# A graph layer with gathered node rows: five selected tiles in the odd groups, and gathers released by the selection products alone

## The chip, the cores and the metric

The kernel runs on one core of a Trainium2 chip. The metric is the device time of one execution in microseconds (us). The core has a matrix engine (PE, whose weight loads the profile lists apart as PEld), a vector engine (DVE), a scalar engine (ACT), a general engine (POOL), which here only issues indirect loads, and a queue engine (SP) that issues the plain loads and stores. PE writes its products to PSUM; DVE and ACT read them from there.

## The reference, cut to what matters

There are N = 6250 nodes with F = 64 features, and E = 200,000 edges sorted by their destination. Each edge takes the features of its source node, weighs them by nine numbers from a small network on its attributes, goes through a 64 x 9 x 64 tensor, and is summed at its destination; the sum is scaled and shifted by a second small network, added to the node's features and normalised.

```python
w = jax.nn.silu(edge_attr @ W1 + b1) @ W2 + b2
h_src = features[src]
msg = jnp.einsum('ef,em,fmg->eg', h_src, edge_sh * w, W_tp)
agg = jax.ops.segment_sum(msg, dst, num_segments=N) / jnp.sqrt(jnp.float32(AVG_DEG))
emb = jax.nn.silu(c_noise[:, None] @ Wn1 + bn1) @ Wn2 + bn2
gamma, beta = jnp.split(emb, 2, axis=-1)
x = _layernorm(features + agg * (1.0 + gamma) + beta, axis=-1)
```

## The kernel before

The edges lie in tiles of 128, one edge per partition, and 16 tiles make a group; there are 98 groups, numbered 0 to 97. The main loop (L859) runs over i and works on several groups at once: it brings the rows of the source nodes for group i + 2, selects rows for group i + 1, and sums group i into its destinations.

The rows `features[src]` of a tile reach the tile's place in `hs` in one of three ways.

- **Gathered:** an indirect load on POOL (L125), one per tile. This is how most tiles come.
- **Row by row:** in every fourth group from 7 on (`SPG`), the first tile comes by 128 single-row loads on SP (L143).
- **Picked:** the last `picked(g)` tiles of a group are selected on PE from a copy of all node features that lies on the chip. DVE builds a 128 x 896 table of zeros and ones from the tile's keys (`hot_k`, L653, in `hots`); PE multiplies it with the features in 14 products, seven slices times two halves of the number (`pxw`, L668, in `pick`); DVE keeps the right one of seven columns by a masked multiply (`xm`, L678) and a reduction (L681). There are three PSUM tiles for `pxw` and seven tiles for `hot_k`. The keys are loaded with room for five tiles in every group (`Q` = 5), whether or not five are picked.

Between the first pick of group i + 1 and its other picks stand **the small products** (`middle`, L805): the first layer of the edge network for group i + 2 (`hidden`, L594), its second layer for group i + 1 (`second`, L618), in odd i the projection of a pair of groups (`project`, L760), and the products of the gathered rows with the edge weights for group i (`windows`, L708). For odd i from 3 on, `place` (L775) adds two products that put sums at their nodes inside the first pick. Their PSUM tile is the one that `second` writes next, after ACT (`carry`, L781) and DVE (`yt`, L784) have read it. So an odd i is an iteration in which an even group is picked, and it holds more small products; an even i picks an odd group.

The order on each engine is the program's own order. Gathers are set by hand: `beats(i + LEAD, units)` shares the gathers of group i + 2 evenly over a number of units, and `beat(u, mm)` counts u units when a product has been issued; whenever the count passes the next mark, one gather is issued on POOL that waits for just that product. A product of a pick counts 1, and the small products count 4.5 (`hidden`), 3.4 (`second`), 12 (`project`) and 3.3 for every four products of `windows`. The units of an iteration are 14 per picked tile plus 21 in even i and 33 in odd i. What is left at the end of an iteration is issued without a wait (`beats_end`). A gather's wait needs a notice from PE, an update of PE's semaphore that the product carries; ACT and DVE wait on notices of the same semaphore.

Of the kernel before, what the change touches and what calls it, by code (L numbers as in the profile page):

```python
# [22 lines left out]
NBLK = (NT + KB - 1) // KB  # L23
# [5 lines left out]
LEAD = 2  # L29
LB = 2  # L30
Q = 5
J = 7
# [19 lines left out]

def picked(g):

    return Q - 2 if g in (0, NBLK - 1) else Q - (g % 40 != 30)


def tiles(g):
    return min(KB, NT - g * KB)
# [9 lines left out]
def gnn_resnorm_kernel(ctx: ExitStack, tc: tile.TileContext, x, src, dst, dst_row, ea, sh, cn,  # L69
# [18 lines left out]
    with ExitStack() as fast:  # L88
# [495 lines left out]
        def hidden(g, act=True, beside=None):  # L584

            e = ea_t.pop(g)
            p1 = psum.tile([P, 2, 4 * P], F32, tag="p1", name=f"p1_{g}")
            p1_t[g] = p1
            if beside:
                beside(p1[:, :, 2 * P:])  # L590
            half = [p1[:, 0, 0:2 * P], p1[:, 1, 0:2 * P], pzw[0][:, 2 * P:], pzw[1][:, 2 * P:]]
            for s in range(2):
                for q in range(4):
                    mm = nc.tensor.matmul(half[q][s * H:(s + 1) * H].rearrange("p (c t e) -> p c t e", c=4, t=2),  # L594
                                     w1bd[q * D:(q + 1) * D, (q % 2) * H:(q % 2 + 1) * H],
                                     e[q * D:(q + 1) * D].rearrange("p (s t c e) -> p s c t e", s=2, t=2, c=4)[:, s],
                                     start=True, stop=True)
            beat(4.5, mm)
            st[g] = work.tile([P, 4, 2 * P], F32, tag="st", name=f"st{g}")
            if act:  # L600
                hidden_act(g)
# [11 lines left out]
        def second(g):  # L613

            s = st.pop(g)
            p2[g] = psum.tile([P, 2, 2 * P], F32, tag="s", name=f"p2_{g}")
            for c in range(KB // 4):
                mm = nc.tensor.matmul(p2[g][c * D:(c + 1) * D, 0, :].rearrange("p (q e) -> p q e", q=4), w2p,  # L618
                                 s[:, :, c * 2 * D:(c + 1) * 2 * D], start=True, stop=True)
            beat(3.4, mm)  # L620
            p2s[g] = work.tile([P, 2 * P], F32, tag="p2s", name=f"p2s{g}")
            nc.scalar.activation(p2s[g], p2[g][:, 0, :], AF.Identity, bias=b2c)  # L622

# [65 lines left out]
        def windows(g, k0s=None, last=None):  # L689

            nk = tiles(g)
            end = g == NBLK - 1
            hsg, ag = hs[g], a[g]
            z = zs[g] if g in zs else sums(g)


            for k0 in range(0, nk, ZT) if k0s is None else k0s:
                n = min(ZT, nk - k0)
                k1 = 0
                if last is not None:  # L700
                    n, k1 = (n, n - 1) if last else (n - 1, 0)
                pz = [pzw[k0 // ZT][:, 0:ZT // 2 * M * W].rearrange("p (k m w) -> p k m w", m=M, w=W)] * 2
                if end and last is not False:
                    pe = px_next()[:, 0:ZT // 2 * M * W].rearrange("p (k m w) -> p k m w", m=M, w=W)
                    pz = [pe if last else pz[0], pe]
                for k in range(k1, n):
                    v = k % 2
                    mm = nc.tensor.matmul(pz[v][v * F:(v + 1) * F, k // 2].rearrange("p m w -> p (m w)"),  # L708
                                          hsg[:, k0 + k, :], ag[:, k0 + k].rearrange("p m w -> p (m w)"),
                                          start=True, stop=True)  # L710
                    if k % 4 == 3:
                        beat(3.3, mm)
                    if k0 + k == 0:

                        for d in hs_dma.pop(g)[(g not in SPG):]:
                            tc.add_manual_dep(mm.ins, d.ins.name, mybir.DependencyInfo(
                                mybir.DependencyClass.Sync, mybir.DependencyReason.DATA), reason="rows of the group")
                for v in range(2):
                    for h in range(2):
                        k = k1 + (v - k1) % 2  # L720
                        if k >= n:
                            continue
                        copy = nc.vector.tensor_copy if last is False else nc.scalar.copy
                        copy(  # L724
                            z[h * F:(h + 1) * F, 0:5 - h, k0 + k:k0 + n:2, :].rearrange("p m k w -> p k m w"),
                            pz[v][v * F:(v + 1) * F, k // 2:(n + 1 - v) // 2, h:M:2, :])
# [19 lines left out]
        def project(q, pt=None):  # L746
# [11 lines left out]
            for c in range(5):  # L758
                for h in range(2):
                    mm = nc.tensor.matmul(pt[h * F:(h + 1) * F], wtc2[:, c, :], z[h][:, c], start=(c == 0), stop=(c == 4))  # L760
            beat(12, mm)
            rt = work.tile([P, KW], F32, tag="rt", name=f"rt{q}")

            def turn(rp):
# [86 lines left out]
        with tc.manual_schedule(), tc.tile_pool(name="temp", bufs=1) as temp:  # L851
# [7 lines left out]
            for i in range(1, NBLK):  # L859
# [13 lines left out]
                    tables.pop()()  # L873
                while stores:
                    stores.pop(0)()
                beats(i + LEAD, 2 * J * picked(i + 1) + (21 if i % 2 == 0 else 33))
                more = []
                if i + 2 < NBLK:
                    more = [lambda: hots(i + 2, 0, 2)]
# [30 lines left out]
            g = NBLK - 1  # L910
# [258 lines left out]
```

## Time and profile before

| | |
|---|---|
| time, median of 3 runs | 1808.46 us (1806.99 to 1809.7) |
| profiled execution, its own time | 1810.38 us |
| its span, first to last instruction | 1808.5 us |
| mean granted TensorE clock | 0.953 |
| busy: PE / PEld / DVE / ACT / POOL | 1588.4 / 1338.5 / 1252.2 / 512.8 / 1090.0 us |
| picked tiles | 392, of 14 products each |
| gathers | 1148 |

A row of the costliest groups reads: line, engine, operation, output and input, shapes and count; behind the first bar the busy time in us and the mean of one in ns; behind the second the idle time of the engine just before these instructions, and what ended it. The ends of matmuls are modelled by the profiler, not observed. "Issue" is idle time for which the profile shows no wait, and "remote" is a wait that was ended by an update which the profile can't give to an instruction. In the view by stretches, PEclk is the granted TensorE clock as a share of full speed. In the timeline a row gives the start in us, the length in us of the merged run, the engine, and in brackets the idle time before it.

### The profile page before, as it was taken

How to read it: one execution, taken by the hardware profiler on the slowest of the kernel's cores; microseconds unless marked ns; L12 is line 12 of the kernel's file. 1: busy time of each engine (PE TensorE's matmuls, PEld its weight loads, DVE VectorE, ACT ScalarE, POOL GpSimd, SP SyncE). 2: the span in 40 equal slices, each digit the busy share in tenths (PEclk: the TensorE clock that was granted, in tenths of full speed). 3: DMA queues.
4: the chain of work that ended last, by engine and by line, in shares of the span. 5: the costliest groups of instructions: out<-in, count | busy, mean ns of one | idle time of the engine just before them, and what ended most of it. 6: DMA issues, size and time to landing. Idle time of an engine off the chain costs nothing.

```text
span 1808.5 us, 38434 instructions
## 1 busy us (share of the span) xinstructions
PE 1588.4 (88%) x12330; PEld 1338.5 (74%) x12330; DVE 1252.2 (69%) x2249; ACT 512.8 (28%) x1435; POOL 1090.0 (60%) x1157
## 2 busy tenths in 40 slices
PE   5888989899989988988899888988989899888988
PEld 4777878677767777777777777777877677776876
DVE  6677777667667677676776777767767666667676
ACT  3322323232223132323231323232313232222232
POOL 6566566566666666666666666666666666665662
PEclk8899999999999999999999999999999999999999
DMA  5411122112112212122112111211122112211210
GB/s 164 95 46 48 47 71 49 46 49 71 46 49 47 70 49 48 48 69 48 47 47 68 46 47 45 69 45 47 46 66 48 45 46 50 63 47 46 67 24 18
DMA packets 89767, 98.89 MB, mean 55 GB/s; under 512 B 36548, under 2 KB 51094, under 8 KB 89558
## 3 DMA queue, kind: packets, MB, share of 16 engines
q0 software_dynamic: 36736, 37.69, 10.9%
q1 hardware_dynamic: 52246, 57.06, 10.3%
q8 instruction: 100, 1.64, 0.4%
q10 hardware_dynamic: 576, 1.61, 0.2%
q14 instruction: 109, 0.89, 0.2%
HBM read 94.50 MB, written 1.75 MB: 53 GB/s over the span
## 4 chain that ended last, share of the span: by engine, by line
PE 81%; issue 11%; DVE 6%; DMA 1%; another core or an unknown queue 1%; ACT 0%; SPq 0%; POOL 0%; DVEq 0%; ACTq 0%; POOLq 0%
PE pxw L668 59%; PE pzw L708 8%; PE p L760 5%; PE p L618 4%; PE p L594 2%; DVE xm L678 2%; DVE hs L681 1%; PE ps L775 0%; PE p L790 0%; PE p L813 0%; DVE hot_k L653 0%; DMA hs<-in_x_dram,src_i 0%; DVE mean L978 0%; PE p L765 0%
## 5 line engine op out<-in xcount | busy, mean ns | idle before, releaser
L125 POOL DMA_INDIRECT hs<-in_x_dram,src_i x1148 | 1088.8, 948 | 694.7 <-PE pxw L668 224.7
L668 PE MATMUL pxw<-xs_w,hot_k 128*128 128x448 f32 x5488 | 1184.4, 371 | 34.0 <-issue 20.8
L668 PEld LDWEIGHTS pxw<-xs_w,hot_k 128*128 128x128 f32 x5488 | 1030.7, 191 | 136.6 <-issue 51.5
L678 DVE SCALAR_TENSOR_TENSOR xm<-li,jl,pxw 128x448 f32<-128x448 f32 x392 | 265.7, 678 | 418.0 <-PE pxw L668 324.8
L653 DVE TENSOR_TENSOR hot_k<-kr,pxw 128x896 fp32r<-128x896 f16 x385 | 407.1, 1078 | 0.0
L724 ACT COPY ztw<-pzw 64x140 f32<-64x140 f32 (+1 forms) x778 | 208.9, 269 | 155.9 <-PE pxw L668 81.7
L681 DVE TENSOR_REDUCE hs<-xm 128x64 f32<-128x448 f32 x392 | 243.1, 620 | 13.8 <-issue 0.3
L622 ACT ACTIVATE p2s<-p,b2c 128x256 f32<-128x256 f32 x98 | 46.4, 473 | 718.0 <-remote 261.2
L708 PE MATMUL pzw<-a,hs 128*64 128x63 f32 x3116 | 160.0, 246 | 65.6 <-issue 62.8
L708 PEld LDWEIGHTS pzw<-a,hs 128*64 128x64 f32 x3116 | 138.9, 157 | 102.3 <-issue 97.0
L618 PE MATMUL p<-st,w2p 128*32 128x256 f32 x784 | 86.5, 403 | 72.1 <-issue 47.0
L638 DVE TENSOR_TENSOR a<-oh,p 128x1008 f32<-128x1008 f32 x98 | 117.9, 1203 | 3.3
L760 PE MATMUL p<-ztw,wtc 128*64 128x112 f32 x940 | 89.0, 322 | 33.2 <-issue 32.1
L760 PEld LDWEIGHTS p<-ztw,wtc 128*64 128x64 f32 x940 | 67.6, 172 | 67.6 <-issue 67.4
L618 PEld LDWEIGHTS p<-st,w2p 128*32 128x32 f32 x784 | 20.4, 109 | 123.3 <-issue 93.3
L609 ACT ACTIVATE st<-pzw,b1c 128x256 f32<-128x256 f32 x196 | 82.3, 470 | 3.6 <-PE pxw L668 1.7
L605 ACT ACTIVATE st<-p,b1c 128x512 f32<-128x512 f32 x98 | 67.0, 683 | 28.9 <-PE pzw L708 11.5
L781 ACT COPY carry<-ps 128x128 f32<-128x128 f32 x48 | 12.4, 258 | 208.7 <-PE pzw L594 93.9
L594 PE MATMUL pzw<-ea,w1bd 32*64 32x256 f32 x784 | 67.0, 399 | 1.0 <-issue 0.9
L594 PE MATMUL p<-ea,w1bd 32*64 32x256 f32 x784 | 66.1, 400 | 0.0
L629 DVE STREAM_TRANSPOSE p<-p2s 128x256 f32<-128x256 f32 x98 | 44.4, 453 | 10.9 <-issue 7.8
L633 DVE TENSOR_TENSOR p<-p,sh 128x72 f32<-128x72 f32 x196 | 47.2, 241 | 6.7
(176 smaller groups left out, 508.3 us busy)
## 6 DMA issues: line engine op xcount, KB each, us to landing
hs<-in_x_dram SPq DMA_DIRECT2D x2944, 0.2 KB
ea<-in_ea_dram SPq DMA_DIRECT2D x48, 512.0 KB
hs<-in_x_dram,src_i POOLq DMA_INDIRECT x1148
kr<-kd SPq DMA_DIRECT2D x48, 320.0 KB
sh<-in_sh_dram SPq DMA_DIRECT2D x49, 144.0 KB
cb<-cn_d SPq DMA_DIRECT2D x12, 128.0 KB
out_dram<-o SPq DMA_DIRECT2D x23, 64.0 KB
dst_i<-in_dst_dram SPq DMA_DIRECT2D x1, 768.0 KB
```

Of the source, the lines that this page charges most:

```text
L125: d = nc.gpsimd.indirect_dma_start(out=hs[g][:, t - g * KB, :], out_offset=None, in_=x, in_offset=bass.IndirectOffsetOnAxis(ap=src_i[:, t: ...
L594: mm = nc.tensor.matmul(half[q][s * H:(s + 1) * H].rearrange("p (c t e) -> p c t e", c=4, t=2), w1bd[q * D:(q + 1) * D, (q % 2) * H:(q % 2 ...
L609: nc.scalar.activation(st[g][:, 2 + q], pzw[q][:, 2 * P:], AF.Silu, bias=b1c)
L618: mm = nc.tensor.matmul(p2[g][c * D:(c + 1) * D, 0, :].rearrange("p (q e) -> p q e", q=4), w2p, s[:, :, c * 2 * D:(c + 1) * 2 * D], start= ...
L638: nc.vector.tensor_mul(a[g], oh_t.pop(g)[:, :, None, :].to_broadcast([P, KB, M, W]), sw.unsqueeze(3).to_broadcast([P, KB, M, W]))
L653: nc.vector.tensor_tensor(hot_k[g, t], keys[:, t, None, :].to_broadcast([P, J, P]), n_p.unsqueeze(2).to_broadcast([P, J, P]), op=ALU.is_equal)
L668: mm = nc.tensor.matmul(px.rearrange("p f l -> p (f l)"), hot_k[g, t][:, h, :], xs[i][:, h].rearrange("p f l -> p (f l)"), start=(h == 0 a ...
L678: nc.vector.scalar_tensor_tensor(xm, li[:, None, :].to_broadcast([P, F, J]), jl[:, c:c + 1], px, op0=ALU.is_equal, op1=ALU.mult)
L681: read_by[g, t] = nc.vector.tensor_reduce(hs[g][:, tiles(g) - q + t, :], xm, AX.X, ALU.add)
L708: mm = nc.tensor.matmul(pz[v][v * F:(v + 1) * F, k // 2].rearrange("p m w -> p (m w)"), hsg[:, k0 + k, :], ag[:, k0 + k].rearrange("p m w ...
L724: copy(z[h * F:(h + 1) * F, 0:5 - h, k0 + k:k0 + n:2, :].rearrange("p m k w -> p k m w"), pz[v][v * F:(v + 1) * F, k // 2:(n + 1 - v) // 2 ...
L760: mm = nc.tensor.matmul(pt[h * F:(h + 1) * F], wtc2[:, c, :], z[h][:, c], start=(c == 0), stop=(c == 4))
```

## The change

Two things change. First, the number of picked tiles: every odd group from 3 to 95 has five instead of four, and groups 30 and 70, which had five, have four. That is 47 tiles more and 2 fewer. Second, the pacing of the gathers: the four calls of `beat` behind small products go, and the units of an iteration are those of the picks alone, 14 per picked tile.

```diff
 def picked(g):

-    return Q - 2 if g in (0, NBLK - 1) else Q - (g % 40 != 30)
+    return Q - 2 if g in (0, NBLK - 1) else Q - (g % 2 == 0 or g == 1)
...
                                      start=True, stop=True)
-            beat(4.5, mm)
             st[g] = work.tile([P, 4, 2 * P], F32, tag="st", name=f"st{g}")
...
                                  s[:, :, c * 2 * D:(c + 1) * 2 * D], start=True, stop=True)
-            beat(3.4, mm)
             p2s[g] = work.tile([P, 2 * P], F32, tag="p2s", name=f"p2s{g}")
...
                                           start=True, stop=True)
-                    if k % 4 == 3:
-                        beat(3.3, mm)
                     if k0 + k == 0:
...
                     mm = nc.tensor.matmul(pt[h * F:(h + 1) * F], wtc2[:, c, :], z[h][:, c], start=(c == 0), stop=(c == 4))
-            beat(12, mm)
             rt = work.tile([P, KW], F32, tag="rt", name=f"rt{q}")
...
-                beats(i + LEAD, 2 * J * picked(i + 1) + (21 if i % 2 == 0 else 33))
+                beats(i + LEAD, 2 * J * picked(i + 1))
```

## The prediction

> **What bounds the kernel now.** I read the page's busy times and its chain first, then the costliest groups, the timeline of one group, and stretches of equal make-up against each other.
>
> ```profile
> span 1808.5 us, 38434 instructions
> PE 1588.4 (88%) x12330; PEld 1338.5 (74%) x12330; DVE 1252.2 (69%) x2249; ACT 512.8 (28%) x1435; POOL 1090.0 (60%) x1157
> ...
> PE 81%; issue 11%; DVE 6%; DMA 1%; another core or an unknown queue 1%; ACT 0%; SPq 0%; POOL 0%; DVEq 0%; ACTq 0%; POOLq 0%
> ...
> L125 POOL DMA_INDIRECT hs<-in_x_dram,src_i x1148 | 1088.8, 948 | 694.7 <-PE pxw L668 224.7
> L668 PE MATMUL pxw<-xs_w,hot_k 128*128 128x448 f32 x5488 | 1184.4, 371 | 34.0 <-issue 20.8
> ...
> L678 DVE SCALAR_TENSOR_TENSOR xm<-li,jl,pxw 128x448 f32<-128x448 f32 x392 | 265.7, 678 | 418.0 <-PE pxw L668 324.8
> L653 DVE TENSOR_TENSOR hot_k<-kr,pxw 128x896 fp32r<-128x896 f16 x385 | 407.1, 1078 | 0.0
> ...
> L681 DVE TENSOR_REDUCE hs<-xm 128x64 f32<-128x448 f32 x392 | 243.1, 620 | 13.8 <-issue 0.3
> ...
> L708 PE MATMUL pzw<-a,hs 128*64 128x63 f32 x3116 | 160.0, 246 | 65.6 <-issue 62.8
> ...
> L618 PE MATMUL p<-st,w2p 128*32 128x256 f32 x784 | 86.5, 403 | 72.1 <-issue 47.0
> ...
> L760 PE MATMUL p<-ztw,wtc 128*64 128x112 f32 x940 | 89.0, 322 | 33.2 <-issue 32.1
> ```
>
> PE sets the end: the chain lies on it for 81%, another 11% is "issue" and most of that is PE's, and POOL has none of it. PE's idle time sits at the small products: 65.6 + 72.1 + 33.2 = 170.9 us in front of L708, L618 and L760. In front of the picks there are 34.0 us. POOL waits for PE; it is ahead of it by more than a group.
>
> What ends those idle times? The timeline of an even group (32) shows it.
>
> ```profile
> 605.31 0.94 POOL L125 DMA_INDIRECT hs<-in_x_dram,src_i  x1 [1.28 <-PE pxw L668]
> ...
> 606.49 0.28 PE L775 MATMUL ps<-c,r 112*128 112x256 f32 x1
> ...
> 606.55 0.94 POOL L125 DMA_INDIRECT hs<-in_x_dram,src_i  x1 [0.30 <-issue]
> 606.61 2.16 PE L668 MATMUL pxw<-xs_w,hot_k 128*128 128x448 f32 x10
> ...
> 609.63 0.27 ACT L781 COPY carry<-ps 128x128 f32<-128x128 f32 x1 [8.25 <-PE pzw L594]
> 609.93 0.29 DVE L784 TENSOR_TENSOR yt<-ps,carry 128x128 f32<-128x128 f32 x1 [1.83 <-ACT carry L781]
> ...
> 610.30 0.94 POOL L125 DMA_INDIRECT hs<-in_x_dram,src_i  x1 [0.30 <-issue]
> ...
> 612.48 0.39 PE L618 MATMUL p<-st,w2p 128*32 128x256 f32 x1 [1.00 <-issue]
> 612.60 0.68 DVE L678 SCALAR_TENSOR_TENSOR xm<-li,jl,pxw 128x448 f32<-128x448 f32 x1 [0.39 <-remote]
> ...
> 618.81 10.40 PE L668 MATMUL pxw<-xs_w,hot_k 128*128 128x448 f32 x51 [0.86 <-issue]
> ```
>
> The product of L775 ends at 606.77 by the profile, but its reader on ACT, idle for 8.25 us, starts at 609.63: 2.9 us late. The pick's last product ends at 608.77; its reader on DVE starts at 612.60, 3.8 us late. From 605.31 to 611.24 gathers ran without a break, one every 1.25 us (0.94 plus 0.30 between). So I read: **while gathers follow each other closely, PE's notices reach the other engines late**, what waits for them is late, and PE stops among the small products, where dependent steps are short and many. That is a reading, not shown.
>
> The stops cost clock too. These are stretches of four groups, each from the first pick of a group of number 4k + 1 to that of 4k + 5; the columns are the length, the busy times with their counts, the granted clock and the DMA.
>
> ```profile
> 481.10:555.30 74.20, 65.66 (x507) 54.98 (x507) 50.86 (x92) 21.05 (x58) 44.78 (x48) 0.98 0.25 66
> 555.30:626.30 71.00, 65.06 (x522) 56.31 (x522) 52.82 (x95) 20.73 (x58) 43.45 (x47) 0.98 0.18 40
> 626.30:700.70 74.40, 64.99 (x507) 54.57 (x506) 50.85 (x92) 21.05 (x58) 45.33 (x48) 0.98 0.26 65
> ...
> 1206.90:1279.10 72.20, 64.48 (x500) 54.00 (x499) 49.47 (x85) 20.25 (x57) 44.68 (x48) 0.95 0.19 45
> 1279.10:1352.90 73.80, 65.77 (x513) 56.71 (x512) 51.73 (x87) 20.12 (x57) 44.49 (x48) 0.95 0.22 52
> 1352.90:1423.70 70.80, 63.34 (x499) 52.88 (x499) 48.84 (x83) 20.25 (x57) 43.60 (x47) 0.98 0.22 52
> ```
>
> The second and the fifth hold groups 30 and 70, with a fifth pick each: some 14 products more and a gather fewer. They took 71.0 and 73.8 us, mean 72.4; their four neighbours 74.2, 74.4, 72.2 and 70.8, mean 72.9. There the fifth pick was free, give or take 1.5 us. The groups around the first of them, one by one (29 to 32):
>
> ```profile
> 555.30:571.20 15.90, 14.83 (x120) 12.89 (x120) 11.65 (x22) 5.49 (x14) 9.50 (x11) 1.00 0.13 26
> 571.20:591.20 20.00, 18.03 (x152) 16.08 (x152) 16.97 (x32) 6.60 (x17) 12.25 (x13) 1.00 0.13 24
> 591.20:605.50 14.30, 14.18 (x117) 12.09 (x115) 11.42 (x21) 4.08 (x13) 8.69 (x10) 1.00 0.37 104
> 605.50:626.30 20.80, 18.02 (x137) 15.25 (x138) 12.79 (x21) 4.56 (x14) 13.02 (x14) 0.92 0.12 23
> ```
>
> Group 30 kept the full clock, group 32 has 0.92, and 31 has 0.1 us idle against 29's 1.1. Over the span the clock is 0.953, so about 0.047 x 1808.5 = 85 us were lost to it, start and end included. Idle small products and clock together are 171 + 85 = 256 us: the most that calmer small products can return.
>
> **The change part by part.** *Picks.* 47 odd groups gain one, groups 30 and 70 lose one: 45 x 14 = 630 products. A pick that runs unhindered takes 14 x 10.40/51 = 2.86 us (the last row of the timeline); the mean over all is 1184.4/392 = 3.02. Nothing hides them, for PE is the path: **45 x 2.86 = +129 us**, at most 136.
>
> *DVE* gets 45 x (1.078 + 0.678 + 0.620) = 107 us. At 2.38 us against PE's 2.86 per pick it keeps up, hidden behind the pick itself; without that cover it would be the 107 us. The keys of five tiles are already loaded; no plain transfer is added. All seven `hot_k` tiles are now taken in an odd group: the next table waits for the pick before, which DVE has by then waited for anyway, so nothing.
>
> *Gathers.* 45 go, 45 x 0.948 = 43 us of POOL, worth nothing directly, since POOL isn't on the path.
>
> *Pacing.* Before, an even i shared 12 gathers over 77 units and an odd i 11 or 12 over 89: inside picks one per 6.4 units or 1.31 us, and one per 7.4 to 8.1 units, 1.5 to 1.65 us; 54 of 166 units of such a pair lay in small products. Now it is 12 over 70 units, 1.19 us, and 10 or 11 over 56, 1.04 to 1.14 us. All are below POOL's 1.25 us. A pair has 22.5 gathers, 28.1 us on POOL, against nine picks of 25.7 us; so released gathers queue on POOL and run on into the small products that were to be kept free of them. Behind a waiting gather stand only further gathers, and their reader `windows` comes more than an iteration later; that cover is ample. What it can return lies between 0, if the queue fills the small products as before, and all 256 us. The nearest row, the fifth pick of group 30, returned its whole price, but its iteration released a gather every 103/11 = 9.4 units, 1.9 us, wider than before, where the change goes narrower than POOL can follow. So I take a third, about the share of units that lay in small products (54/166): **-85 us**. Below 0 it can go as well: if picks had to follow POOL, 28.1 - 25.7 = 2.4 us a pair, 47 times, is +113.
>
> A notice itself has a price in the Trainium skill, "TensorE: Matmul & The Clock Gate", section "The cost: per-tile semaphore tail": increments serialize, at 26.3 ns each. By that alone, some four notices a group fewer at small products would return about 98 x 4 x 0.026 = 10 us, an estimate, and the time would be near that of the second rival. The trace's readers that start 2.9 and 3.8 us late say that more than this hangs on them.
>
> *Sum*, on the profiled execution's own 1810.4 us (span 1808.5): 1810.4 + 129 - 85 = 1854. It lies 1.9 above the median of the runs, so I predict **1852 us**, +2.4%.
>
> **The rivals.** *The small products become calm* (faster). The mechanism is the late notice; its place L618, L760 and L708; it decides once the idle and clock returned pass 129 of the 256 us. For it: the five-pick row of group 30 and the row of 31. Were each pair like them, it would take 14.3 + 2.86 for the odd group and 20.0 - 2.86 for the even one, 34.3 us, against (74.2 + 71.0)/4 = 36.3: 47 x 2.0 = 94 us less, 1716. With two pairs of three, 1808 - 62 = **1746**. Against it: the queue on POOL.
>
> The Trainium skill, "Perfetto Trace Analysis", section "Identifying the Most-Contended Engine", says that PE's headroom is to be judged by weight loads, not by matmul busy time. By that rule PE at 74% has room for the picks, as this rival needs; the trace agrees with it in the two five-pick stretches alone.
>
> *The full price* (slower by more). Gathers jam the small products as before, and nothing returns: 1808 + 129 = **1937**; each 2.4 us per pair that picks must follow POOL comes on top. For it: 1.04 to 1.19 us between releases, below 1.25. Against it: the queue empties in the longer small products of odd i.
>
> *A wash.* The fifth pick is free everywhere, as in the two stretches, and the pacing neither helps nor harms: **1808**. Then the change does not do what its second part says.
>
> **How the numbers follow.** Forecast 0.48 (its own range 1820 to 1890), calm 0.20, full price 0.19, wash 0.13. A measurement of this kernel tells about 0.2% from no change. Faster: 0.20 and a quarter of the wash, 0.23. Same: 0.07. Slower: 0.48 + 0.19 and the rest of the wash, 0.70. The range 1765 to 1940 leaves out some two thirds of the calm case and a third of the full price, in all 2 in 10.
>
> **What would show it.** 437 picks, 6118 products and 1103 gathers must stand in the groups. L668's busy time should grow by 129 to 136 us. The forecast needs idle in front of L708, L618 and L760 near 115 us in place of 171, and a clock near 0.965; the calm case needs idle below 80 and 0.98; the full price leaves 171 and 0.953, and adds to L668's 34.0 us of idle. Rows of gathers at 1.25 us that go on past the first of the small products show the queue on POOL. If DVE's wait in front of L678 (418 us) vanishes, DVE has become the bound and I was wrong on it; if readers of PE start on time while gathers run closely, the reading of the notices is wrong.

## The result, and the profile after

The changed kernel takes **1903.37 us** (median; 1900.02 to 1911.71) against 1807.72 us (1803.67 to 1809.7) for the kernel before beside it: ratio 1.0539, interval 1.0497 to 1.0581. It is slower by 95.65 us. I had forecast 1852 us, 44 us slower: the sign was right, the size less than half of it.

First the busy times and the costliest groups of the profile after (line numbers are up to five lower than before: L666 is the picks' product, L617 `second`, L706 `windows`, L756 `project`).

```profile
span 1898.2 us, 39766 instructions
PE 1695.6 (89%) x12960; PEld 1451.4 (76%) x12960; DVE 1352.8 (71%) x2384; ACT 504.6 (27%) x1435; POOL 1044.3 (55%) x1112
...
L125 POOL DMA_INDIRECT hs<-in_x_dram,src_i x1103 | 1043.0, 946 | 830.8 <-PE pxw L666 533.2
L666 PE MATMUL pxw<-xs_w,hot_k 128*128 128x448 f32 x6118 | 1296.1, 370 | 12.9 <-ACT pxw L369 9.9
...
L706 PE MATMUL pzw<-a,hs 128*64 128x63 f32 x3116 | 156.4, 244 | 65.9 <-issue 63.1
...
L756 PE MATMUL p<-ztw,wtc 128*64 128x112 f32 x940 | 99.1, 280 | 81.7 <-issue 70.6
...
L617 PE MATMUL p<-st,w2p 128*32 128x256 f32 x784 | 65.9, 391 | 21.9 <-issue 11.7
```

The counts are as announced: 6118 products, 1103 gathers. PE is busy for 107.2 us more (1695.6 - 1588.4) and idle for 17.5 us less (1898.2 - 1695.6 = 202.6 against 1808.5 - 1588.4 = 220.1); the span grew by 89.7. The idle time in front of the small products only moved: 65.9 + 81.7 + 21.9 = 169.5 us against 170.9. `second` lost 50 us of it, `project` gained 48. The clock rose from 0.953 to 0.966, which is 64.5 us lost in place of 85.

The waits of the other engines:

```profile
ACT p2s L620 <- remote: 610.7, 74, 14.6
POOL hs L125 <- PE pxw L666: 533.2, 351, 7.4
DVE xm L676 <- PE pxw L666: 292.8, 197, 4.9
ACT carry L776 <- PE pxw L666: 225.5, 30, 12.9
```

The chain of waits breaks off after 5% of the span and can't be read. The last row says that the reader of `place`, in 30 iterations, was set free, as the profile infers it, only when a later pick product was already done. So notices still come late. Where ACT stood idle for `place`, it starts its reader 1.6 us after the product in the median, against 3.5 us in the trace before. The reader of `second` on ACT, L620, starts 2.9 us after its product in the median, against 2.2 us before. (The medians of this reader, here and below, leave out the first 100 us.) The groups 29 to 32, from first pick to first pick, in the order of the prediction's rows:

```profile
577.90:597.40 19.50, 17.66 (x134) 15.62 (x133) 15.81 (x33) 5.66 (x15) 11.17 (x12) 1.00 0.17 39
597.40:615.80 18.40, 16.42 (x138) 13.81 (x138) 11.45 (x19) 6.41 (x16) 9.47 (x11) 1.00 0.12 23
615.80:634.30 18.50, 17.45 (x131) 15.15 (x130) 14.89 (x26) 4.08 (x13) 11.41 (x13) 1.00 0.29 84
634.30:655.60 21.30, 18.94 (x138) 16.07 (x137) 12.70 (x20) 4.55 (x14) 10.38 (x11) 0.84 0.19 50
```

29 and 31 have the fifth pick now and take 19.50 and 18.50 us in place of 15.90 and 14.30. Group 32 is again the one with the low clock, 0.84.

### The profile page after: what moved, and what is told of

The parts are those of the page before. It is cut to its first block, busy times and chain, and to the rows that moved or that the text cites. A ratio compares the mean times of both kernels' runs of the same rounds, so it can differ in the third digit from the quotient of the medians.

```text
span 1898.2 us, 39766 instructions
## 1 busy us (share of the span) xinstructions
PE 1695.6 (89%) x12960; PEld 1451.4 (76%) x12960; DVE 1352.8 (71%) x2384; ACT 504.6 (27%) x1435; POOL 1044.3 (55%) x1112
## 3 DMA queue, kind: packets, MB, share of 16 engines
HBM read 93.03 MB, written 1.75 MB: 50 GB/s over the span
## 5 line engine op out<-in xcount | busy, mean ns | idle before, releaser
L125 POOL DMA_INDIRECT hs<-in_x_dram,src_i x1103 | 1043.0, 946 | 830.8 <-PE pxw L666 533.2
L666 PE MATMUL pxw<-xs_w,hot_k 128*128 128x448 f32 x6118 | 1296.1, 370 | 12.9 <-ACT pxw L369 9.9
L666 PEld LDWEIGHTS pxw<-xs_w,hot_k 128*128 128x128 f32 x6118 | 1156.3, 192 | 101.8 <-ACT pxw L369 10.0
L676 DVE SCALAR_TENSOR_TENSOR xm<-li,jl,pxw 128x448 f32<-128x448 f32 x437 | 296.2, 678 | 380.7 <-PE pxw L666 292.8
L651 DVE TENSOR_TENSOR hot_k<-kr,pxw 128x896 fp32r<-128x896 f16 x430 | 455.8, 1078 | 0.0
L679 DVE TENSOR_REDUCE hs<-xm 128x64 f32<-128x448 f32 x437 | 271.0, 620 | 15.1
L620 ACT ACTIVATE p2s<-p,b2c 128x256 f32<-128x256 f32 x98 | 46.4, 473 | 828.2 <-remote 610.7
L706 PEld LDWEIGHTS pzw<-a,hs 128*64 128x64 f32 x3116 | 131.0, 154 | 112.2 <-issue 105.4
L706 PE MATMUL pzw<-a,hs 128*64 128x63 f32 x3116 | 156.4, 244 | 65.9 <-issue 63.1
L756 PE MATMUL p<-ztw,wtc 128*64 128x112 f32 x940 | 99.1, 280 | 81.7 <-issue 70.6
L756 PEld LDWEIGHTS p<-ztw,wtc 128*64 128x64 f32 x940 | 61.8, 141 | 117.8 <-issue 117.0
L617 PE MATMUL p<-st,w2p 128*32 128x256 f32 x784 | 65.9, 391 | 21.9 <-issue 11.7
L594 PE MATMUL pzw<-ea,w1bd 32*64 32x256 f32 x784 | 75.0, 402 | 4.3 <-issue 4.0
L617 PEld LDWEIGHTS p<-st,w2p 128*32 128x32 f32 x784 | 16.8, 108 | 65.9 <-issue 45.9
L497 DVE TENSOR_SCALAR gam<-p 128x64 f32<-128x64 f32 x49 | 11.0, 224 | 77.8 <-ACT st L604 77.8
```

The source lines that it names most:

```text
L125: d = nc.gpsimd.indirect_dma_start(out=hs[g][:, t - g * KB, :], out_offset=None, in_=x, in_offset=bass.IndirectOffsetOnAxis(ap=src_i[:, t: ...
L651: nc.vector.tensor_tensor(hot_k[g, t], keys[:, t, None, :].to_broadcast([P, J, P]), n_p.unsqueeze(2).to_broadcast([P, J, P]), op=ALU.is_equal)
L666: mm = nc.tensor.matmul(px.rearrange("p f l -> p (f l)"), hot_k[g, t][:, h, :], xs[i][:, h].rearrange("p f l -> p (f l)"), start=(h == 0 a ...
L676: nc.vector.scalar_tensor_tensor(xm, li[:, None, :].to_broadcast([P, F, J]), jl[:, c:c + 1], px, op0=ALU.is_equal, op1=ALU.mult)
L679: read_by[g, t] = nc.vector.tensor_reduce(hs[g][:, tiles(g) - q + t, :], xm, AX.X, ALU.add)
```

## The experiments

One fact has to stand first, for without it the numbers can't be read: **the kernel before does not take the same time on every chip.** It took 1808 us where the result was measured and 1835 us on the chip of the first four experiments, but 1455.0, 1455.2, 1456.6 and 1455.1 us on the four chips of the later ones. Each ratio below is against the kernel before on the same chip. I call the first two the chips with late notices and the other four the prompt ones; why, the traces show. The word chip is a short form here: each of the five chips on record was met once, the chip of the result is not on record, and the two measurements with late notices are also the two earliest, so a state that changed with time isn't told apart from the chip.

### On a chip with late notices: the parts one by one

**Picks alone** (five in odd groups, pacing of before):

```diff
-    return Q - 2 if g in (0, NBLK - 1) else Q - (g % 40 != 30)
+    return Q - 2 if g in (0, NBLK - 1) else Q - (g % 2 == 0 or g == 1)
```

> Five picks in the odd groups, the pacing of before (small products release gathers too). Theory A, late notices (gathers that follow each other closely hold PE's notices back, and the stops of PE at the small products and the lost clock come from that): an even i releases 12 gathers over 91 units, 1.55 us apart, wider than before, so part of the price of 129 us comes back: 1840 to 1890 us. Theory B, PE's own stops (the idle time at the small products belongs to these products, whatever the gathers do): the full price, 1808 + 129 = 1937 us, and the changed pacing is what gave 34 us back.

**Pacing alone** (four picks as before, the other hunks of the change):

```diff
-            beat(4.5, mm)
...
-            beat(3.4, mm)
...
-                    if k % 4 == 3:
-                        beat(3.3, mm)
...
-            beat(12, mm)
...
-                beats(i + LEAD, 2 * J * picked(i + 1) + (21 if i % 2 == 0 else 33))
+                beats(i + LEAD, 2 * J * picked(i + 1))
```

> The picks of before, gathers released by picks alone: 11 or 12 over 56 units, 0.95 to 1.04 us apart. Theory A: closer than POOL's 1.25 us, a queue that runs on into the small products, so the idle time there stays and notices within picks come later: 1808 to 1840 us. Theory B: pacing is worth nothing or what calm small products return, 1775 to 1808 us. If the two parts add up, this run and the one with the picks alone must together make the 96 us of the change.

**The fifth pick in even groups** in place of odd ones, pacing of before:

```diff
+    return Q - 2 if g in (0, NBLK - 1) else Q - (g % 2 == 1 or g < 3)
```

> Five picks in the even groups from 4 to 96 in place of the odd ones, 437 picks in all as in the changed kernel, the pacing of before. Theory A: as in the two five-pick stretches, where the fifth pick of an even group was free because its 11 gathers lie 1.9 us apart and the clock holds: 1800 to 1840 us. Theory B: 45 times 2.86 us whichever groups have it, 1937 us.

Before: 1834.55 us. Picks alone: **1773.42**, ratio 0.9666 (0.965 to 0.9682). Pacing alone: **2048.49**, ratio 1.1157 (1.1134 to 1.118). Even groups: 1787.95, ratio 0.9744 (0.9728 to 0.976). All three lie outside what either theory had expected: picks alone and even groups came out faster than both, pacing alone much slower than both. First the picks alone, costliest groups and then the stretch of groups 29 to 32; after them the pacing alone:

```profile
span 1771.7 us, 39742 instructions
PE 1636.6 (92%) x12960; PEld 1407.6 (79%) x12960; DVE 1353.1 (76%) x2384; ACT 506.4 (29%) x1435; POOL 1049.4 (59%) x1112
...
L668 PE MATMUL pxw<-xs_w,hot_k 128*128 128x448 f32 x6118 | 1286.8, 366 | 26.0 <-issue 12.5
...
L708 PE MATMUL pzw<-a,hs 128*64 128x63 f32 x3116 | 145.5, 229 | 62.6 <-issue 61.1
...
L760 PE MATMUL p<-ztw,wtc 128*64 128x112 f32 x940 | 68.3, 267 | 16.4 <-issue 15.0
...
L618 PE MATMUL p<-st,w2p 128*32 128x256 f32 x784 | 64.0, 391 | 15.1 <-issue 9.0
```

```profile
539.50:609.60 70.10, 66.77 (x535) 58.11 (x534) 54.05 (x96) 20.70 (x58) 42.10 (x45) 1.00 0.20 53
```

```profile
span 2045.7 us, 38461 instructions
PE 1726.7 (84%) x12330; PEld 1455.3 (71%) x12330; DVE 1254.2 (61%) x2249; ACT 507.3 (25%) x1435; POOL 1092.0 (53%) x1157
...
L666 PE MATMUL pxw<-xs_w,hot_k 128*128 128x448 f32 x5488 | 1240.4, 386 | 9.8 <-ACT pxw L369 5.5
...
L706 PE MATMUL pzw<-a,hs 128*64 128x63 f32 x3116 | 214.0, 278 | 150.8 <-issue 148.3
```

So **the two parts of the change work against each other**. With 630 products more the kernel got 61 us faster: `project` and `second` hardly wait (16.4 + 15.1 us), though `windows` still does (62.6 us), and the clock is at 0.989. The pacing alone costs 214 us: 150.8 us idle in front of `windows`, and a clock of 0.889, which is 227 us of 2045.7 lost.

The kernels stand in the order of their releases' narrowest spacing; by the mean, the last two are level. By the units of the code and 0.204 us for a product (the 10.40/51 of the prediction), even i and odd i have:

| kernel | even i | odd i | ratio |
|---|---|---|---|
| pacing alone | 0.95 us | 0.95 to 1.04 us | 1.1157 |
| the change (chip of the result) | 1.19 | 1.04 to 1.14 | 1.0539 |
| before | 1.31 | 1.51 to 1.65 | 1 |
| fifth pick in even groups | 1.43 | 1.75 to 1.91 | 0.9744 |
| fifth pick in odd groups | 1.55 | 1.65 to 1.82 | 0.9666 |

POOL needs 1.25 us a gather. Below that, gathers queue on POOL and run in unbroken rows; the wider above it, the more pauses there are. The traces bear this out. Taking gathers less than 0.4 us apart as one row, and what lies after the first 100 us (for the kernel before, the trace of the prediction):

| kernel | gathers in a row, mean | products of `second` that end under a row | their reader starts after the row's last gather, median | reader after product, median of all |
|---|---|---|---|---|
| pacing alone | 3.9 | 89 of 94 | 1.56 us | 4.3 us |
| the change (chip of the result) | 3.9 | 88 of 93 | 1.26 us | 2.9 us |
| before (chip of the result) | 3.1 | 69 of 94 | 1.40 us | 2.2 us |
| fifth pick in even groups | 2.6 | 44 of 93 | 0.89 us | 0.9 us |
| fifth pick in odd groups | 2.8 | 74 of 93 | 1.15 us | 2.1 us |

In the median the reader starts about a microsecond after the row ends, in all five kernels. ACT's own notices aren't late: where DVE stood idle for them, it starts 0.03 us after ACT's `carry` and `p2s` in each of these traces. In the table of spacings the spacing isn't the only thing that differs: the two narrow kernels are also the two that release nothing at small products. The experiment that was to separate these comes below and met prompt chips only.

**Plain loads in the gathers' place.** The same products release the same number of transfers, but from group 8 on each is a plain load of 128 rows on SP; the gathering itself is left out.

```diff
-                d = nc.gpsimd.indirect_dma_start(
+                if g < 8:
+                    d = nc.gpsimd.indirect_dma_start(
...
+                else:
+                    d = nc.sync.dma_start(hs[g][:, t - g * KB, :], x[(t % 40) * P:(t % 40 + 1) * P, :])
```

> From group 8 on each gather on POOL becomes a plain load on SP of 128 consecutive rows, of the same bytes to the same place, released by the same product: the rows are not those of the edges, the gathering itself is left out. Theory A: no indirect loads on POOL, so PE's notices come on time (readers of the place products and of the first pick within 0.3 us), the idle time in front of the small products falls from 171 us to below 60, the clock is above 0.98, and the time is 1560 to 1660 us. Theory B: the idle time and the clock stay, about 1808 us.

It took 1900.59 us, so as a time it missed, and the clock, 0.904, did too: SP's queue filled up and the keys and edge attributes came late (DVE waited 436 us for keys, PE 308 us for attributes). But what it was made for can be read. In front of the small products PE was idle for 9.3 + 6.2 + 1.4 = 16.9 us. Here is who set the reader of `place` free, first in this kernel, then in the changed kernel where the result was measured (us waited, times):

```profile
L784 ACT COPY carry<-ps x48: 245/266/267, 95.6 to 1877.2; 128x128 f32<-128x128 f32 x48
...
  PE ps L778: 171.1, 23
  PE pxw L671: 12.5, 2
```

```profile
  PE pxw L666: 225.5, 30
  PE pzw L594: 98.5, 10
  PE ps L770: 34.9, 6
```

Without gathers the reader starts at its own product, L778, in 23 of the 25 waits; with them in 6 of 46, and in the others at some later product. With the picks alone, on the same chip as the plain loads, it is 4 of 45. The reader of `second` agrees: with plain loads it starts 0.13 us after its product (median), with the picks alone 2.1 us. The stretches of groups 31 to 34 without gathers:

```profile
598.30:615.90 17.60, 14.27 (x116) 12.09 (x115) 11.16 (x21) 4.21 (x13) 0.00 (x0) 1.00 0.26 74
615.90:632.50 16.60, 15.48 (x138) 13.55 (x138) 12.70 (x21) 4.58 (x14) 0.00 (x0) 1.00 0.12 27
632.50:656.40 23.90, 16.12 (x121) 13.64 (x120) 11.61 (x22) 5.51 (x14) 0.00 (x0) 0.86 0.23 67
656.40:672.10 15.70, 15.16 (x138) 13.39 (x137) 14.16 (x29) 6.60 (x17) 0.00 (x0) 1.00 0.12 26
```

The even groups (second and fourth row), which had been the long ones, took 16.60 and 15.70 us with the full clock; the clogged SP hits the odd ones. So on this chip late notices go with the gathers themselves, not with the number of notices sent to release something. Whether POOL's work on a gather does it or the transfer that it starts, this kernel doesn't tell, since its loads are issued by SP.

### On a prompt chip: the price of a pick

**Three picks in odd groups** and **five picks in all groups**:

```diff
+    return Q - 2 if g in (0, NBLK - 1) or (g % 2 == 1 and g > 2) else Q - 1
```

> Three picks in the odd groups from 3 to 95 in place of four: 343 picks in all, 49 fewer than before, and 49 gathers more, with the pacing of before. Theory A, late notices: an odd i releases 12 gathers over 63 units, 1.07 us apart, below POOL's 1.25 us, so more stops and lost clock eat the 49 x 2.86 = 140 us of PE work that are gone, and the time is not shorter: 1800 to 1950 us. Theory B, PE's own stops: 1808 - 140 = 1668 us.

```diff
+    return Q - 2 if g in (0, NBLK - 1) else Q - (g < 3)
```

> Five picks in all groups from 3 to 96, 484 in all, with the pacing of before. Theory A: against the kernel with five in the odd groups alone, 47 x 2.86 = 134 us more of PE work, and of its idle time 1.2 us (even) and 1.0 us (odd) a group are left to be returned, at most 105 us: between the time of before and 3% less than it, slower than the kernel with five in the odd groups. Theory B: 92 x 2.86 = 263 us more than before.

**No gather waits for a product** from group 8 on, and **the notices without the gathers** (a small memset on POOL waits for the product, plain loads on SP bring other rows):

```diff
-                if k == 0 and after is not None:
+                if k == 0 and after is not None and g < 8:
```

> From group 8 on gathers wait for no product, only for a free tile of rows: POOL runs the 11 or 12 of a group one after the other. PE sends 12 notices a group fewer. Theory A: the longest rows of close gathers, so notices come later still, readers wait for the end of the row, idle time and lost clock grow: 1950 us or more. Theory C: fewer notices, faster than before, below 1780 us.

```diff
-                d = nc.gpsimd.indirect_dma_start(
...
+                    d = nc.sync.dma_start(hs[g][:, t - g * KB, :], x[(t % 40) * P:(t % 40 + 1) * P, :])
+                    m = nc.gpsimd.memset(tick, 0.0)
...
-                    tc.add_manual_dep(d.ins, after.ins.name, mybir.DependencyInfo(
+                    tc.add_manual_dep(m.ins, after.ins.name, mybir.DependencyInfo(
```

> From group 8 on POOL fills one number per partition in place of each gather, released by the same product, and the tile comes by a plain load of 128 consecutive rows on SP that waits for no product: PE sends the same notices, POOL answers each, but no indirect load runs; the gathering is left out. Theory A, in the form that the indirect loads hold the notices back: idle time of an even group 2.9 us falls below 0.8, the readers of PE start on time, the clock is above 0.98, 1600 to 1680 us. Theory C, that the number of notices holds PE up, whatever POOL does with them: idle time and time as before, about 1808 us.

The expectations were written for a kernel of 1808 us, and the chip was a prompt one, so these four don't test the theories on late notices; only the full price of the picks, in the kernel with five everywhere, came near one of them (263 us expected, 255.99 measured). Before: 1454.99 us. Three picks: 1515.9, ratio 1.0417 (1.04 to 1.0435). Five everywhere: 1710.98, ratio 1.176 (1.174 to 1.178), which is 255.99/92 = 2.78 us for each pick. No releases: 1454.59. The memsets: 1854.42, again SP's queue (43% of the chain), so that one told nothing about notices. In the kernel with three picks each pick less is a gather more, and the gathers become the limit:

```profile
L125 POOL DMA_INDIRECT hs<-in_x_dram,src_i x1197 | 1133.9, 947 | 366.6 <-DMA hs<-in_x_dram,src_i 188.2
```

1197 gathers at 1.25 us (0.947 and the 0.30 between) are 1496 of its 1515.2 us. With no releases the gathers run 1.25 us apart from end to end, and the reader of `second` starts 0.13 us after its product (median): what the prediction read as a property of the hardware doesn't hold on every chip.

### The change itself on a prompt chip

**The change**, and **the change with the old units**: picks and deleted `beat` calls as in the change, but the units of an iteration keep their + 21 and + 33, so releases in the picks are as wide as with picks alone, and what is left over goes out at the iteration's end.

> The changed kernel itself again, beside the others of this job, because the kernel before took 1808 and 1835 us on two chips and 1455 on a third, where its PE was busy for 99%. Theory A2, late notices that only some chips have: where before takes some 1800 us or more, 1.05 times it, as first measured; where it takes 1455 us, nothing can be returned and the price of 129 us stands, 1575 to 1590 us. Theory B, PE's own stops, has no room for the two kinds of chips.

```diff
-                beats(i + LEAD, 2 * J * picked(i + 1))
+                beats(i + LEAD, 2 * J * picked(i + 1) + (21 if i % 2 == 0 else 33))
```

> The changed kernel with the old counts of units (21 and 33 added) but no release at small products: inside picks the gathers lie as wide apart as with the picks alone changed (1.55 to 1.8 us), none is released at small products, and the 3 or 4 left run without a wait at the end of an iteration. On a slow chip, theory A2: the wide spacing in picks is what counts, so most of the gap between the change and the picks alone is gone: below the time of before. If quiet small products harm in themselves, it is as slow as the change. On a fast chip all are 1575 to 1590 us.

Beside them the kernel without releases once more, and one that keeps all notices (for memsets on POOL) and brings one plain load a group in place of the gathers:

> From group 8 on the gathers of before wait for no product, only for a free tile of rows. On a fast chip it took the time of before (1454.6 us). On a slow chip, theory A2: the closest gathers of all, 1.25 us apart throughout, so notices come latest and the time is 1950 us or more; theory C (the number of notices is what costs): below 1780 us, since PE sends 12 a group fewer.

```diff
...
+                    if not hs_dma[g]:
+                        n = len(due[g]) + 1
+                        hs_dma[g].append(nc.sync.dma_start(
+                            hs[g][:, t - g * KB:t - g * KB + n, :],
+                            x[0:P * n, :].rearrange("(p k) f -> p k f", k=n)))
+                    m = nc.gpsimd.memset(tick, 0.0)
...
```

> From group 8 on POOL fills one number per partition in place of each gather, released by the same product, and one plain load a group on SP, which waits for no product, brings the bytes of all its tiles (rows not those of the edges; the gathering is left out). SP is not filled up as it was with one load a tile. Theory A2: whatever the chip, no indirect loads, no late notices: PE busy 98% or more, clock above 0.99, 1440 to 1470 us. Theory C: on a slow chip as slow as before.

Before: 1455.23 us. The change: **1578.85**, ratio 1.085 (1.0832 to 1.0868), +123.62 us or 2.75 us for each of the 45 picks. Wide: 1578.92, ratio 1.0849 (1.083 to 1.0867). No releases: 1454.23. No gathers: 1454.01. The change here, its costliest groups and then the stretch of groups 29 to 32:

```profile
span 1576.2 us, 39766 instructions
PE 1561.2 (99%) x12960; PEld 1377.3 (87%) x12960; DVE 1347.2 (85%) x2384; ACT 505.4 (32%) x1435; POOL 1046.8 (66%) x1112
...
L125 POOL DMA_INDIRECT hs<-in_x_dram,src_i x1103 | 1045.5, 948 | 506.8 <-PE pxw L666 274.3
...
L706 PE MATMUL pzw<-a,hs 128*64 128x63 f32 x3116 | 110.1, 223 | 0.0
L776 ACT COPY carry<-ps 128x128 f32<-128x128 f32 x48 | 12.8, 266 | 293.1 <-PE ps L770 293.1
...
L756 PE MATMUL p<-ztw,wtc 128*64 128x112 f32 x940 | 55.4, 264 | 0.0
```

```profile
470.80:535.00 64.20, 64.20 (x535) 57.11 (x535) 54.79 (x97) 20.59 (x58) 42.53 (x46) 1.00 0.22 60
```

The program is the same as where the result was measured, a gather takes the same 948 ns, and yet PE has no idle time in front of `windows` and `project`, 0.6 us in front of `second`, and the clock is 0.999. The reader of `place` waits for `place` alone (L770, all of its 293.1 us). The four groups that took 77.70 us there (577.90 to 655.60) take 64.20.

That makes a comparison possible which no edit gives: one program, two traces. They run alike, to within 0.3 us, until about 18 us. Here is the setup, first on the chip of the result, then on the prompt one (start, length, engine, in brackets the idle time before):

```profile
14.15 1.41 POOL L125 DMA_INDIRECT hs<-in_x_dram,src_i  x1 [0.30 <-issue]
...
19.27 0.64 PE L617 MATMUL p<-st,w2p 128*32 128x256 f32 x8
...
24.68 0.23 ACT L392 COPY first_f<-pzw 16x98 f32<-16x98 f32 x1 [7.75 <-remote]
...
30.85 0.94 POOL L125 DMA_INDIRECT hs<-in_x_dram,src_i  x1 [0.30 <-issue]
34.49 0.47 ACT L620 ACTIVATE p2s<-p,b2c 128x256 f32<-128x256 f32 x1 [9.32 <-remote]
...
36.23 0.94 POOL L125 DMA_INDIRECT hs<-in_x_dram,src_i  x1 [4.44 <-DVE nid L408]
```

```profile
19.02 0.64 PE L617 MATMUL p<-st,w2p 128*32 128x256 f32 x8
19.13 0.23 ACT L392 COPY first_f<-pzw 16x98 f32<-16x98 f32 x1 [2.19 <-PE pzw L391]
...
19.73 0.47 ACT L620 ACTIVATE p2s<-p,b2c 128x256 f32<-128x256 f32 x1
...
30.85 0.94 POOL L125 DMA_INDIRECT hs<-in_x_dram,src_i  x1 [0.30 <-issue]
...
32.10 0.95 POOL L125 DMA_INDIRECT hs<-in_x_dram,src_i  x1 [0.30 <-issue]
```

Eight products of L617 end at 19.91 and 19.66 us. On the prompt chip their reader on ACT starts at 19.73. On the other it sits idle for 9.32 us and starts at 34.49, **14.6 us after the product**, and 2.7 us after the row of gathers that had run since 14.15 us broke off at 31.79. None of these early gathers waits for a product. So on that chip a row of gathers holds PE's notices back, whoever releases it, and the pause at its end let this one through; on the prompt chip the same row, gather for gather at the same times, holds back nothing. A pause is not the only way out: within the row ACT's L392 started at 24.68 us, 5.3 us after the product of L391 that sets it free on the prompt chip within 0.03 us, and a reader on DVE started 2.5 us late. In the loop the contrast is the same. Of the changed kernel's products of `second` that end under a row, the reader starts 1.26 us after the row's last gather there, and on the prompt chip 0.70 us before it (medians).

### Two more chips

The kernels that separate spacing, place and number of the releases ran on two more chips; both were prompt. No releases, one load a group and wide spacing are the kernels shown above; the last has three picks in every eighth group.

> The gathers from group 8 on wait for no product and run as closely as they come (1.25 us apart); everything else as before. On a chip where the kernel before takes about 1455 us this changes nothing (1454 to 1455), as on the second and third chips. On one where it takes 1800 us or more: if closely spaced gathers alone make PE's other notices late, whoever releases them, the time rises, to 1900 or over, because no pause is left between gathers. If it is the notices for the gathers themselves, one for each of 1103 gathers, that the others stand behind, the time falls towards 1455.

> The releases of before stay, but from group 8 on each wakes only a small memset on POOL, and one plain load a group puts data in the place of the gathered rows: the gathering is left out, so the values are not the reference's. On a chip at about 1455 us nothing changes. On one at 1800 us or more: if the gathers' own work on POOL (947 ns each) or their transfers make the notices late, it falls to 1455 to 1480; if the notices are slow by themselves, it stays above 1750.

> Five tiles in every odd group from 3 on, with the spacing of before inside the picks and no gather released by small products: between the change (all releases in the picks, 1.04 to 1.19 us apart) and the picks alone. On a chip at about 1455 us it gives 1579 like the change itself. On one at 1800 us or more: if what hurts in the change is the density of releases in the picks, this gives back most of it, 1740 to 1790; if it is that no gather starts under the small products, it stays at 1880 to 1920.

> As g1_no_release: the gathers from group 8 on wait for no product. On a chip where the kernel before takes about 1455 us nothing changes. On one at 1800 us or more: 1900 or over if closely spaced gathers alone make PE's notices late; towards 1455 if the notices sent for the gathers do.

> As g3_wide_in_picks: five tiles in every odd group from 3 on, the spacing of before inside the picks, no gather released by small products. On a chip at about 1455 us: 1578 to 1579, as on the two before. On one at 1800 us or more: 1740 to 1790 if the density of releases in the picks is what hurts in the change, 1880 to 1920 if it is that no gather starts under the small products.

```diff
+    return Q - 2 if g in (0, NBLK - 1) or g % 8 == 5 else Q - (g % 40 != 30)
```

> Three picks in place of four in every eighth group (5, 13, ... 93; 12 groups), so 24 gathers more; all else as before. On a chip at about 1455 us, where PE is 99% busy and each pick cost its full 2.78 us: 12 x 2.78 = 33 us less, 1422, if the gathers in these groups (27 to 29 in place of 13 to 15 at 1.25 us) still come in time; 1440 to 1465 if they don't, as in e4_odd_three, where 1197 gathers at 1.25 us set the time. On one at 1800 us or more, where the added picks gave back more than they cost: slower, by 10 to 30 us.

On the first (before: 1456.57 us): no releases 1455.78, ratio 0.9996 (0.9985 to 1.0007); one load 1454.63; wide 1578.49, ratio 1.0839 (1.0808 to 1.0871). On the second (before: 1455.08): no releases 1454.36; wide 1578.67, ratio 1.085 (1.0828 to 1.0871); few threes 1470.62, ratio 1.0107 (1.009 to 1.0124). The last was expected to win 33 us, or to lie between 1440 and 1465 if gathers came late; it lost 15.5 and missed both. The expectation also miscounted: a pick less is one gather more, 12 here, not 24.

```profile
L125 POOL DMA_INDIRECT hs<-in_x_dram,src_i x1160 | 1098.5, 947 | 355.2 <-DMA hs<-in_x_dram,src_i 179.0
...
L708 PE MATMUL pzw<-a,hs 128*64 128x63 f32 x3116 | 112.6, 226 | 27.7 <-DMA hs<-in_x_dram,src_i 16.6
```

1160 gathers at 1.25 us are 1450 us, and PE begins to wait for them in front of `windows`. So the kernel before stands, on a prompt chip, just where PE (99% busy in the kernel without releases) and POOL (1148 gathers, 1435 us) meet, and neither direction that was tried, more picks or fewer, gave anything.

## Why the prediction was wrong

**What bounds the kernel.** Right where it was measured: PE sets the end, idle at small products, and the stops cost clock. The reading "while gathers follow each other closely, PE's notices reach the other engines late" is shown for those chips by the setup above, by the rows in the loop and by the kernel with plain loads. As a statement on the hardware in general it was wrong: on four chips gathers run 1.25 us apart and readers start on time, which the prediction itself had named as the sign against it.

**The picks' price, 45 x 2.86 = 129 us.** Right. Where PE has no gaps it measured 2.75 us (the change) and 2.78 us (five everywhere). DVE hid its 107 us: it still waits 292.8 us for PE in front of L676 (324.8 before).

**The relief, "a third: -85 us".** This is the step that failed. Where the result was measured, the change returned 129 - 95.65 = 33 us of the 256. And the third was not only too big; it was given to the wrong part. I took the fifth pick as a price and the pacing as the relief. On the chip where both were tried alone the picks made the kernel 61 us faster, so that they returned some 61 + 124 = 185 us (an estimate: 124 is their price on the prompt chip), and the pacing cost 214 us. That the whole came out slower, as forecast, was luck: what I had taken for the price made that kernel faster, and what I had taken for the relief made it slower. The two do not simply add: -61 + 214 would be +153, and +95.65 was measured, though on another chip; the whole change wasn't run beside its parts there, so how far chip or interplay explains this stays open.

The profile had a hint in a row that I quoted. Group 30's fifth pick was free, and I noted that its iteration released a gather every 1.9 us, "wider than before, where the change goes narrower than POOL can follow". Having seen that, I still let the share of units in small products decide. The nearest row spoke of spacing, and by spacing the pacing would harm. My bound on the bad side, +113 us for picks that must follow POOL, named a mechanism that didn't come: idle time before the picks fell from 34.0 to 12.9 us, and was 9.8 us with the pacing alone.

**The rivals.** The calm small products came, in part, with the picks alone: 62.6 + 16.4 + 15.1 = 94.1 us idle, not yet below 80, but a clock above 0.98. "1746" is 62 us less than 1808, and 61 us less was measured at 1835; that the two agree is chance, for the rival's sum had the pacing in it. The case against it, the queue on POOL, is seen in the whole change: 88 of 93 products of `second` end under a row of gathers, 69 of 94 before. The full price, 1937, holds on prompt chips, +124 us, but for another reason: there was nothing to return. The wash did not come.

**What was to show it.** Idle near 115 us in front of the three small products was the forecast's, 171 the full price's: 169.5 was seen. The clock, 0.966, was the forecast's 0.965. L666's busy time grew by 111.7 us, not 129 to 136; the clock's rise by 1.4%, on 1184 us, is about the 17 us between.

**The two rules of the Trainium skill.** The Trainium skill, "TensorE: Matmul & The Clock Gate", section "The cost: per-tile semaphore tail", gives 26.3 ns for each increment. Taking the waits off the gathers from group 8 on leaves 1033 products with a notice where the trace before has 1884, 851 fewer, which would by that rule return up to 22 us, an estimate; 0.4, 1.0, 0.8 and 0.7 us less were measured beside 1454.99, 1455.23, 1456.57 and 1455.08, so no run agrees. The Trainium skill, "Perfetto Trace Analysis", section "Identifying the Most-Contended Engine", has PE's headroom judged by MFU, the share of the peak arithmetic, and by weight loads. On a prompt chip weight loads stood at 87%, and every added pick cost its full 2.75 us: there the trace does not agree either, and the matmuls' 99% was the number to go by.

**What stays open.** Whether it is the narrow spacing or the missing releases at small products that costs the 214 us: the wide kernel ran on three prompt chips, where it equals the change, and on none with late notices. The table of rows and the setup speak for the spacing; that is argued, not shown by an edit. The wide kernel would not have told it cleanly either: what it leaves over runs as a row at the iteration's end, and in its traces all products of `second` after the first 100 us, 92 of 92, end under a row. What makes two measurements differ from four is not known. A gather's time on POOL is the same (945 to 950 ns). One difference stands in the records of semaphore updates. Those of the loads' completions count 8,976 to 10,077 in each trace with gathers on the chips with late notices, 25,715 to 28,194 on the prompt ones, and 25,979 with plain loads on a chip with late notices. The loads' are not alone in this: with late notices and gathers the traces hold 47 to 62% of DVE's updates, 40 to 78% of ACT's and 85 to 93% of PE's, on the prompt chips at least 95% of each. Updates may be joined or held there while gathers run, or only not recorded; ACT's reach DVE on time though half of them are not on record, so a missing record alone is no late notice.

## What to carry to other kernels

Time the unchanged kernel beside every variant, on the same chip: here 45 more picks made the kernel 3% faster on one chip and, with either of two other pacings, 8.5% slower on others, and a tuning that smooths one chip's stalls can be pure loss on the next. When an engine issues back-to-back transfers and readers of another engine start microseconds after their product, compare the releases' spacing with the time of one transfer, and try a wider one before a narrower. Where two edits are made together, price each by the row nearest to it; a sum that gives one of them the cost and the other the gain can have both signs wrong.

On the chips with late notices the picks alone, 1773.42 us, beat both kernels (the kernel before took 1834.55 us there); on the prompt ones nothing tried beat the kernel before by more than 1 us.

## What the runs showed of the hardware

- The same program took 1455 to 1457 us on four chips and 1808 and 1835 us on two others, each repeating within 0.4%; the changed kernel 1578.85 and 1903.37 us. The granted clock, 0.999 against 0.966, is part of it, PE's idle time the greater part: 1576.2 - 1561.2 = 15 us against 202.6.
- A row of gathers 1.25 us apart, from 14.15 to 31.79 us, held a notice of PE back by 14.6 us on one chip and not at all on another. In the loop of the changed kernel the reader of `second` starts 2.9 us after its product on the one and 0.13 us on the other.
- Short stops cost twice: pacing alone raised the idle time at `windows` to 150.8 us, and the clock fell to 0.889, at most another 227 us. With the picks alone it was 0.989, 19 us.
- The clock goes to one half for 3.41 us, at times 6.83. Ahead of each of the 24 such stretches between 100 and 1780 us of the changed kernel, PE had been idle for 0.94 to 2.36 of the 3.41 us before, in pauses none of which was over 1.24 us: the 3.41 us before needn't be empty of work for the next to run at half the clock.
- On the prompt chips 851 notices of PE more or less made no difference beyond 1 us.
